# A two-layer graph attention kernel: step 2's norm, flags and adjacency moved, layer 0's mask behind the sums with u, and one maximum as guard

## The chip, the cores and the metric

The kernel runs on one core of a Trainium2 chip. A core has five engines that run at the same time, each through its own list of instructions in order: TensorE (PE, with its weight loads PEld), VectorE (DVE), ScalarE (ACT), GpSimd (POOL) and SyncE (SP, here only a queue that issues DMA transfers; ACT issues some too). Engines wait for each other by semaphores. The metric is the device time of one execution in microseconds (us), lower is better.

## The reference

The input is x, 64 graphs of 256 nodes with 512 features in float32, and a Boolean adjacency of 256 x 256 for each graph. There are two pre-norm attention layers:

```python
h = jnp.maximum(_layernorm(x, axis=-1), 0.0)
x = x + _L0_gnn_ref(h, adj, Wq, Wk, Wv, Wo, bo)
h = jnp.maximum(_layernorm(x, axis=-1), 0.0)
x = x + _L1_gnn_ref(h, adj, gamma, beta, w_qkv, w_out, b_out)
```

Layer 0 has 4 heads of 64, a score outside the adjacency becomes the lowest float, and a node with no neighbour at all therefore attends evenly to all nodes. Layer 1 has 8 heads of 64, a second layernorm with gamma and beta inside, and a mask of adjacency or identity. Both take a softmax over the allowed nodes and project the heads back to 512 features with a bias. All of it is float32.

## The kernel before

**Steps and tiles.** `fast_path` treats two graphs at a time: 512 rows as NT = 4 tiles of 128 x 512, 32 steps in all. Each step goes through layer 0 and layer 1. In a steady period the second layer of step s is mixed with the first layer of step s + 2 and the end of layer 0 of step s + 1, so that PE always has matmuls.

**Projections by seven products.** A projection (q and k together, v, output) is computed as seven half-size products n = 1 to 7 instead of eight (Strassen and Winograd), in the order `SET = (1, 6, 5, 2, 7, 3, 4)`. A product is accumulated in a PSUM bank by PE (L841 for q and k and layer 1's v, L922 for layer 0's v, L938 for the output). It is then taken out by `evacuate` (ACT L775 for n = 1, L783 for n = 2; DVE L777 for n = 6, L779 for 5, L781 for 7, L785 for 3, L787 for 4) or, for the output, by `accumulate` (ACT L794; DVE L796, L798, L800, L803, L805; and three additions of u on POOL, L809: `SUM_U`). Products 3 and 4 go on in the banks that 5 and 7 have used, after the evacuation of 5 and 7; 2 goes on in the bank of 1. The products need sums of quadrants of the inputs (L404 for the weights, once, by `weight_sum`; L407 to L412 on POOL for h and for the attention's result).

**Attention.** PE makes the scores of a pair of heads (L994), DVE adds the mask (L1017), ACT takes the exponential (L1022). No maximum is subtracted. Keys lie on the partitions, so the sums over keys are made in steps: POOL adds the two halves of the keys (`key_halves`, L1029, into the single buffer pd), DVE transposes in 32 x 32 blocks (L1035) and reduces (L1042), then transposes the result (L1095) and sums and inverts (`key_sums`, L1103, L1106). The inverse sums are written to DRAM as a line (SP, L1113) and read back broadcast into the output's tile (SP, `inverse_in`, L1124); PE weighs the values (L1065, L994) and POOL multiplies by the inverse (`normalise`, L1142).

**Guard.** The softmax without a maximum is safe if no sum and no inverse is too large. `key_sums` writes one number for each unit of two pairs of heads into `extremes`; after the last step its overall maximum is compared with a limit, and a slower `general_path` runs only if it is exceeded. L1107 makes that number: a `tensor_tensor_reduce` that adds sums and inverses and takes the maximum, which appears as a custom instruction and a read of the accumulator (97 times).

**Norm and adjacency of layer 0.** `norm0` takes mean and variance of a tile of x on DVE (L615, L616); POOL then makes the scale and the shift of each row (L648, `row_scales` L625 to L627), and ACT applies them (`scale_row`, L631). `norm1` and `norm1_rest` do the like for layer 1 (L615/L616 twice, ACT L672/L673, POOL L688, L689, L625 to L627). h is transposed for PE by DVE in 32 x 32 blocks (`turn_blocks`, L724) and by 16 DMA transfers on SP (`move_blocks`, L736), then copied into place by ACT (L747); the first and some last steps do this on PE (L700, L706).
From step 2 on, the adjacency bytes are packed by POOL (`adjacency_pack`, L532, 3.08 us) and transposed by DVE (`adjacency_turn`, L540, 16 instructions of 0.235 us). `neighbours` (DVE, L559, two) finds the nodes that have a neighbour, `neighbours_line` (DVE, L568, four) turns these flags into a row, and `neighbours_spread` (SP, L575, three transfers) spreads it to all partitions. `mask0` (POOL, L549 and twice L602, 3.4 us) makes the mask of layer 0 from the transposed adjacency and the flags, `mask1` (L549 and twice L610) that of layer 1.

**The order of the work.** It is written out by hand. Every piece is put in a list by `at(period, place, fn, ...)`, the list is sorted by period and place, and the pieces are emitted in that order, so each of PE, DVE, ACT and POOL executes its instructions in that order. A period is 6.4 units of place (6.2 for those before the first, `FIRST`), one unit being about 15 us. An instruction that waits holds up all that stand behind it on its engine. Most places are the same in every step; steps 0, 1 and 2 have places of their own, since in the warm-up (the first 190 us or so) the weights are also transposed by PE (L468, copied by L473) and their sums made (L404: four each of wqk, wo0 and wo1, of wqkv's Q, K and V, and of wv).

Tiles come from pools with a tag and a number of buffers. A tile that reuses a buffer waits until its former content has been read. Which tag a tile has therefore also sets when a load can start.

Of the kernel before, what the change touches and what calls it, by code (L numbers as in the profile page):

```python
# [8 lines left out]
FP = mybir.dt.float32  # L9
# [4 lines left out]
ALU = mybir.AluOpType  # L14
# [301 lines left out]
def fast_path(  # L316
# [19 lines left out]
    nc = tc.nc  # L336
    P = 128
    B, N, D = x.shape
    DH = 64
    G = 2  # L340
    NSTEP = B // G
    NIC = N // P
    NT = G * NIC
# [9 lines left out]
    act = ctx.enter_context(tc.tile_pool(name="act", bufs=1))  # L353
    sm = ctx.enter_context(tc.tile_pool(name="sm", bufs=2))
# [64 lines left out]
    wo0 = const.tile([P, NB, HP0, HD], FP, name="wo0")  # L419
    wqkv1 = const.tile([P, NB, HC, 3, H1], FP, name="wqkv1")  # L420
# [92 lines left out]
    both = act.tile([P, 2, NIC, P, NT], U8, name="both")  # L513
# [99 lines left out]
    def moments(mv, src, t):  # L613
        bs = stat.tile([P, 6], FP, name="bs")
        nc.vector.bn_stats(bs, src[:, t, :])  # L615
        nc.vector.bn_aggr(mv[:, t, 0:2], bs)  # L616
# [47 lines left out]
    def norm1(s, k):  # L664
        st, x1, t = S[s], S[s]["xt"], NORM1[k]
        if k == 0:
            st["mv"] = stat.tile([P, NT, 3], FP, name="mv1", bufs=2)
            st["mean"] = stat.tile([P, NT, 2], FP, name="mg", bufs=2)
            st["h"] = act.tile([P, NT, D], FP, name="h", tag="h" if by_tensor(s, 1) else "turned")
        mv, h = st["mv"], st["h"]  # L670
        moments(mv, x1, t)
        nc.scalar.mul(mv[:, t, 2:3], mv[:, t, 0:1], -1.0)  # L672
        nc.scalar.activation(h[:, t, :], x1[:, t, :], AF.Relu, bias=mv[:, t, 2:3])  # L673
# [40 lines left out]
    def by_tensor(s, lyr):  # L714

        return s == 0 or s == (1, NSTEP - 1)[lyr]
# [262 lines left out]
    units = [0]  # L979
# [108 lines left out]
    def turn_sums(s, lyr, prs):  # L1088

        st = S[s]  # L1090
        part = st.pop(("part", lyr, prs))[:, :len(prs)].rearrange("p i b -> p (i b)")
        nb = 32 * len(prs)
        keys = sm.tile([P, 7, 2 * 32], FP, name="keys", tag="turned_p", bufs=1)[:32, :, :nb]
        for k in range(4):
            nc.vector.transpose(keys[:, k], part[32 * k:32 * (k + 1)])  # L1095
        st["keys", lyr, prs] = keys

    def key_sums(s, lyr, prs):

        st = S[s]  # L1100
        keys = st.pop(("keys", lyr, prs))
        sums, inv, both = (keys[:, k] for k in (4, 5, 6))
        nc.vector.tensor_reduce(  # L1103
            sums, keys[:, :4].rearrange("b k q -> b q k"), axis=mybir.AxisListType.X, op=ALU.add
        )
        nc.vector.reciprocal(inv, sums)  # L1106
        nc.vector.tensor_tensor_reduce(  # L1107
            out=both, in0=sums, in1=inv, scale=1.0, scalar=0.0, op0=ALU.add, op1=ALU.max,
            accum_out=extremes[:32, units[0]:units[0] + 1],
        )  # L1110
        units[0] += 1
        line = st["line", lyr, prs] = dram.tile([len(prs), 2, T], FP, name="line")
        nc.sync.dma_start(  # L1113
            line.rearrange("i e (b q) -> (e b) i q", q=32), inv.rearrange("b (i q) -> b i q", q=32)
        )
# [36 lines left out]
    def at(period, place, fn, *args):  # L1152
        events.append((period * (PERIOD if period >= 0 else FIRST) + place, len(events), fn, args))
# [68 lines left out]
    AT_X, AT_C0, AT_QK, AT_Q0, AT_V0, AT_H1, AT_Z = 2.0, 3.0, 3.5, 4.5, 5.5, 6.06, 6.2  # L1222
# [8 lines left out]
    p = NSTEP - 2  # L1231
# [9 lines left out]
    FIRST_C0, FIRST_Q0, FIRST_V0, FIRST_H1 = 3.0, 3.64, 4.64, 5.2  # L1241
# [5 lines left out]
    for s in range(NSTEP):  # L1247

        p = s - 2
        if s == 1:  # L1250
            p -= 3.93 / FIRST
        at(p - 1 if s != 1 else -2, 3.2 if s == 1 else 5.7 if s < 3 else AT_H1 + 0.01, load_h, s)
        at(p - 1 if s != 1 else -2, 3.2 if s == 1 else 5.7 if s < 3 else 1.3, load_adjacency, s)
        if s < 2:
            at(p, (2.0, 2.4)[s], adjacency_cast, s)
            at(p, (FIRST_Q0 + 0.1425, 3.583)[s], adjacency_transpose, s)
        else:
            at(*((p, 0.45) if s == 2 else (p - 1, 4.9)), adjacency_pack, s)
        for t in range(NT):
            at(p, (0.5 + 0.4 * t, 1.95 + 0.1395 * t)[s] if s < 2 else (0.95, 1.05, 1.2, 1.35)[t], norm0, s, t)  # L1260
            if s == 0:
                at(p, 0.95 + 0.4 * t, first_scale, t)
            else:
                at(p, (2.6 + 0.1 * t, 2.35 + 0.001 * t)[s - 1] if s < 3 else 1.6 + 0.001 * t, scale_row, s, t)
            if not by_tensor(s, 0):
                at(p, AT_X - 0.00035 + 0.00001 * t if s > 2 else (2.6, 2.601, 2.72, 2.721)[t], turn_blocks, s, 0, t)
        if not by_tensor(s, 0):
            at(p, AT_X - 0.00031 if s > 2 else 3.0, move_blocks, s)
        for g in range(G):
            if s < 3:  # L1270
                at(p, (1.8, 2.7, 0.1)[s] + 0.001 * g, neighbours, s, g)
            else:
                at(p - 1, AT_Q0 - 0.0009, neighbours, s, g)
        if s < 2:
            at(p, (2.9, 2.72)[s], neighbours_rows, s)
            at(p, (FIRST_Q0 + 0.285, 3.59)[s], neighbours_turn, s)
        else:
            at(p, 2.3 if s == 2 else 0.05, neighbours_line, s)
            at(p, 2.31 if s == 2 else 0.051, neighbours_spread, s)
        for a in range(NQ if s > 1 else 0):  # L1280
            place = (2.05, 2.2, 2.86, 2.9)[a] if s == 2 else AT_X - 0.00031 if a > 2 else 1 + (a + 4) / 7 - 0.0005
            at(p, place, adjacency_turn, s, a)
        at(p, (FIRST_Q0 + 0.3, 3.74)[s] if s < 2 else 3.1, mask0, s)
        at(p, (FIRST_Q0 + 0.31, 4.43)[s] if s < 2 else 5.85, mask1, s)
        if s == 0:
            at(p, FIRST_C0, first_transposes)
        else:
# [9 lines left out]
        if s < 2:  # L1297
            for t in range(NT):
                place = (FIRST_V0 + 0.14 * t - (0 if t else 0.0005), (4.31, 5.02, 5.16, 5.31)[t])[s]
# [7 lines left out]
        p = s - 1  # L1307
# [20 lines left out]
        for k in range(NT):  # L1328
            at(p, ((2.901, 3.041, 3.181, 3.321), (2.99919, 2.99933, 2.99947, 2.99961), (3.79, 3.8, 3.94, 3.95))[edge][k], norm1, s, k)
            at(  # L1330
                p, ((3.042, 3.182, 3.322, 3.323), (2.99948, 3.2, 3.3, 3.45), (4.08, 4.22, 4.23, 4.37))[edge][k],
                norm1_rest, s, k,
            )
            at(*((0, 3.6 + 0.001 * k), (p, 6.5 + 0.1 * k), (p, 5.6 + 0.01 * k))[edge], second_bias, s, k)
            place = ((3.6112, 3.6113, 3.7502, 3.7503)[k], 3.6 + 0.01 * k, AT_Q0 + (-0.0002, -0.00019, 0.0002, 0.00021)[k])[edge]
            at(p, place, scale_row, s, NORM1[k])
            if edge == 2:
                at(p, AT_Q0 + (0.15, 0.16, 0.29, 0.3)[k], turn_blocks, s, 1, NORM1[k])
# [8 lines left out]
        p = s  # L1347
        if s < NSTEP - 1:
# [3 lines left out]
            p, place = (s + 1, 1.0) if s < NSTEP - 2 else (s, LAST_QK + 2)  # L1352
# [5 lines left out]
        else:  # L1358
            p = s - 1
# [15 lines left out]
    at(-3, 5.71, lambda: gbr.append(first_weights()))  # L1375
    for i in range(4):
        at(-2, 3.01, weight_sum, nc.vector, wqk0, i)
        at(0, 0.9, weight_sum, nc.gpsimd, wo0, i)
    for n, (p, place) in enumerate(((-2, 4.0), (-2, 4.0), (-1, 0.0), (-1, 1.1))):
        at(p, place, lambda n=n: blocks.update({n: weight_load(n)}))  # L1380
    at(-2, FIRST_V0 + 0.2, lambda: gamma_beta(gbr[0]))
    for i in range(16):

        place = (
            *(3.3 - 3.93 + (1 + k) / 7 - 0.0005 for k in range(7)), 0.5205,
            *(0.53 + 0.14 * (k + 1) - 0.0005 for k in range(4)), *(FIRST + (2 + k) / 7 - 0.0005 for k in range(4)),
        )[i]
        at(-1, place, lambda i=i: weight_block(blocks[i // 4], i // 4, i % 4))
    for i in range(4):
        at(-1, 0.1 + 0.01 * i, weight_sum, nc.vector, wqkv1[:, :, :, 0, :], i)  # L1390
        at(-1, 0.54 + 0.0001 * i, weight_sum, nc.gpsimd, wqkv1[:, :, :, 1, :], i)
        at(0, 0.65, weight_sum, nc.gpsimd, wqkv1[:, :, :, 2, :], i)
        at(0, (4.7, 4.701, 4.702, 5.55)[i], weight_sum, nc.gpsimd, wo1, i)
        at(0, 3.61, weight_sum, nc.gpsimd, wv0, i)
# [54 lines left out]
```

## Time and profile before

| | us |
|---|---|
| median of 3 runs | 3095.58 (3095.57 to 3095.6) |
| profiled execution, own time | 3096.28 |
| its span | 3094.5 |
| PE busy | 3072.8 (99%) |
| DVE busy | 2555.7 (83%) |
| POOL busy | 2301.9 (74%) |
| ACT busy | 1207.2 (39%) |

The span is the time from the first to the last instruction in the trace. TensorE had its full clock throughout. In a line of the timeline the columns are start, busy time, engine, line, operation, output and inputs by the program's names, their sizes, the number of instructions taken together (x), and in brackets the idle time of the engine ahead of it and what ended it. In the view of waits the columns are total, times and longest.

### The profile page before, as it was taken

Reading aid. Unit: us, or ns where it says so; the run is one execution under the profiler, and the core shown is the slowest. Engines: PE = TensorE matmul, PEld = TensorE weight load, DVE = VectorE, ACT = ScalarE, POOL = GpSimd, SP = SyncE. Lnnn points to the kernel's source line nnn. Section 1 sums busy time; section 2 is a strip of 40 time slices with the busy share of each in tenths; the row PEclk is TensorE's granted clock in tenths of the full one; section 3 lists DMA queues with packets and bytes.
Section 4 is the critical chain, followed back from the end, with each engine's and each line's share of the span. In section 5 each row is a group of like instructions: output and inputs, shape, how many; then the busy total and the mean of one; then the engine's idle time right before and its main releaser. Section 6 shows DMA issues by size and latency. Waiting matters only on the chain.

```text
span 3094.5 us, 55510 instructions
## 1 busy us (share of the span) xinstructions
PE 3072.8 (99%) x20122; PEld 2528.8 (82%) x20122; DVE 2555.7 (83%) x4851; ACT 1207.2 (39%) x2136; POOL 2301.9 (74%) x2128
## 2 busy tenths in 40 slices
PE   9999999999999999999999999999999999999998
PEld 7778888888888888888888888888888888888887
DVE  6888888888888888888888888888888888888766
ACT  4424343343433344343434334343334444343431
POOL 7887876777777878778787777777787877778753
PEclk9999999999999999999999999999999999999999
DMA  4232222331323322223323233132232222331311
GB/s 140 62 94 80 74 83 74 100 94 54 91 73 92 94 71 79 80 79 94 93 61 88 72 97 94 56 92 73 89 94 80 74 83 73 101 92 53 92 34 50
DMA packets 187591, 251.22 MB, mean 81 GB/s; under 512 B 58088, under 2 KB 78192, under 8 KB 187312
## 3 DMA queue, kind: packets, MB, share of 16 engines
q1 hardware_dynamic: 123776, 179.93, 20.0%
q10 hardware_dynamic: 63536, 67.68, 7.5%
q8 instruction: 162, 2.65, 0.4%
q14 instruction: 117, 0.96, 0.1%
HBM read 128.59 MB, written 34.34 MB: 53 GB/s over the span
## 4 chain that ended last, share of the span: by engine, by line
PE 93%; POOL 3%; DVE 3%; DMA 1%; issue 1%; ACT 0%; SPq 0%; ACTq 0%; DVEq 0%; POOLq 0%
PE mm L841 36%; PE mm L938 17%; PE mm L922 11%; PE sc L994 8%; PE mm L888 6%; PE sc L1065 6%; PE mm L1065 5%; PE mm L994 2%; POOL pd L1029 1%; PE mm L871 1%; DMA h<-blocks 0%; PE mm L964 0%; DVE bs L615 0%; DMA out_dram<-xt 0%; POOL xt L809 0%
## 5 line engine op out<-in xcount | busy, mean ns | idle before, releaser
L841 PE MATMUL mm<-hT,wqkv 128*128 128x256 f32 x3584 | 789.6, 380 | 2.9 <-DVE qk L781 2.1
L841 PEld LDWEIGHTS mm<-hT,wqkv 128*128 128x128 f32 x3584 | 677.1, 190 | 107.2 <-issue 11.8
L1029 POOL TENSOR_TENSOR pd<-p 128x512 f32<-128x512 f32 x383 | 479.3, 1273 | 254.7 <-ACT p L1022 199.1
L938 PE MATMUL mm<-wo,oT 128*128 128x256 f32 x2632 | 579.1, 379 | 1.4 <-DVE v L787 1.2
L938 PEld LDWEIGHTS mm<-wo,oT 128*128 128x128 f32 x2632 | 499.5, 190 | 71.2 <-POOL xt L510 1.5
L1022 ACT ACTIVATE p<-p 128x512 f32<-128x512 f32 x766 | 440.9, 626 | 122.9 <-DVE p L1017 111.4
L1017 DVE TENSOR_TENSOR p<-sc,n 128x512 f32<-128x512 f32 x579 | 363.0, 682 | 111.5 <-PE sc L994 111.5
L841 PE MATMUL mm<-hT,wqk 128*128 128x256 f32 x1792 | 399.0, 382 | 0.0
L922 PE MATMUL mm<-wqkv,hT 128*128 128x256 f32 x1792 | 396.0, 381 | 1.0 <-DVE v L779 0.6
L922 PEld LDWEIGHTS mm<-wqkv,hT 128*128 128x128 f32 x1792 | 337.6, 190 | 57.1 <-issue 10.3
L841 PEld LDWEIGHTS mm<-hT,wqk 128*128 128x128 f32 x1792 | 338.5, 191 | 55.7 <-issue 10.3
L994 PE MATMUL sc<-qk 64*128 64x256 f32 x2320 | 294.7, 385 | 2.2 <-DVE p L1017 2.2
L809 POOL TENSOR_TENSOR xt<-xt,u 128x512 f32<-128x512 f32 x183 | 230.5, 1273 | 66.8 <-DVE xt L798 37.4
L994 PEld LDWEIGHTS sc<-qk 64*128 64x128 f32 x2320 | 218.3, 186 | 63.8 <-issue 27.9
L1035 DVE STREAM_TRANSPOSE turned_p<-pd 128x1024 f32<-128x1024 f32 x192 | 237.1, 1235 | 33.7 <-POOL pd L1029 33.7
L631 ACT ACTIVATE h<-h,mr,r 128x512 f32<-128x512 f32 x252 | 187.6, 803 | 169.8 <-POOL mr L627 169.8
L1142 POOL TENSOR_TENSOR oT<-oT 128x512 f32<-128x512 f32 x188 | 239.9, 1276 | 0.1
L1042 DVE TENSOR_REDUCE part<-turned_p 128x32 f32<-128x1024 f32 x192 | 233.2, 1214 | 4.4
L1065 PE MATMUL sc<-p,v 128*32 128x256 f32 x3152 | 190.8, 382 | 0.0
L888 PE MATMUL mm<-hT,wv 128*128 128x256 f32 x840 | 188.5, 382 | 0.2 <-ACT vT L775 0.2
L794 ACT COPY u<-mm 128x512 f32<-128x512 f32 x62 | 36.3, 585 | 369.9 <-PE mm L938 218.5
L888 PEld LDWEIGHTS mm<-hT,wv 128*128 128x128 f32 x840 | 156.6, 190 | 27.3 <-ACT vT L775 6.6
(155 smaller groups left out, 4458.3 us busy)
## 6 DMA issues: line engine op xcount, KB each, us to landing
h<-blocks SPq DMA_DIRECT2D x960, 64.0 KB, 2.0
oT<-line SPq DMA_DIRECT2D x376, 128.0 KB, 3.0
h<-in_x_dram SPq DMA_DIRECT2D x31, 1024.0 KB, 7.5
xt<-in_x_dram ACTq DMA_DIRECT2D x60, 512.0 KB, 4.3
out_dram<-xt SPq DMA_DIRECT2D x31, 512.0 KB, 3.1
out_dram<-xt ACTq DMA_DIRECT2D x31, 512.0 KB, 4.4
v<-values ACTq DMA_DIRECT2D x480, 32.0 KB, 1.9
ne<-ne SPq DMA_DIRECT2D x90, 64.0 KB, 2.0
```

The source lines that it names most:

```text
L841: nc.tensor.matmul(bank[:, k, :], w[:, wa, c, k, a * P:(a + 1) * P], st["hT"][:, ba, c, :], start=first and (k, c) == (0, 0), stop=(k, c) ...
L888: nc.tensor.matmul(bank, wv0[:, wa, c, :], st["hT"][:, ba, c, :], start=first and c == 0, stop=c == HC - 1, skip_group_check=True,)
L922: nc.tensor.matmul(bank[:, t, :], st["hT"][:, ba, c, t * P:(t + 1) * P], wqkv1[:, wa, c, 2, :], start=first and (t, c) == (0, 0), stop=(t, ...
L938: nc.tensor.matmul(bank[:, t, :], oT[:, ba, c, t * P:(t + 1) * P], w[:, wa, c, :], start=first and (t, c) == (0, 0), stop=(t, c) == (NIC - ...
L994: nc.tensor.matmul(sc[g][e][:, kc, :], qk[rows, 1, k0:k0 + P], qk[rows, 0, g * N:(g + 1) * N], start=True, stop=True,)
L1017: nc.vector.tensor_tensor(p[e][:, g], sc[e], neg[:, :, g, :], ALU.add)
L1022: nc.scalar.activation(p[e][:, g], p[e][:, g], AF.Exp, scale=SCALE)
L1029: nc.gpsimd.tensor_tensor(st["pd"][:, e], p[e][:, :, 0, :], p[e][:, :, 1, :], ALU.add)
L1035: nc.vector.transpose(st["turned_p"], st.pop("pd").rearrange("p e g (b k) -> p (e g b) k", k=32))
L1042: nc.vector.tensor_reduce(st["part", lyr, prs][:, i], st.pop("turned_p"), axis=mybir.AxisListType.X, op=ALU.add)
L1065: nc.tensor.matmul(po[r0:r0 + 32, g, :], (st["v1"][:, g * NIC + kc, pr * P + r0:pr * P + r0 + Q] if lyr else st["v0"][:, r0 // Q, pr, g * ...
L1142: nc.gpsimd.tensor_tensor(dst, dst, invb, ALU.mult)
```

## The change

It has three parts.

1. **Step 2's own preparation for layer 0 takes other places.** Its load of h is issued about one period earlier on SP (for that, layer 1's h of step 0 moves from the tag "h" to the tag "turned"). The four `norm0`, the two `neighbours`, `neighbours_line` and `neighbours_spread`, and 12 of the 16 transposes of `adjacency_turn` on DVE, the row scales, `adjacency_pack` and `mask0` on POOL, and the four `scale_row` on ACT all come earlier in their engines' lists; so does the second mask of step 1. To make room, some weight sums move: the fourth K sum on DVE and on POOL goes later, and those of wo0 come earlier.
2. **Layer 0's mask of steps 3 to 31** (`mask0`, place 3.1) goes to place 3.58, behind the three additions of u (L809) of the step before on POOL.
3. **The guard** takes one `tensor_reduce` with a maximum over sums and inverses together, in place of the `tensor_tensor_reduce` over their sum; its scratch tile has six rows instead of seven.

```diff
-            st["h"] = act.tile([P, NT, D], FP, name="h", tag="h" if by_tensor(s, 1) else "turned")
+            st["h"] = act.tile([P, NT, D], FP, name="h", tag="h" if s == NSTEP - 1 else "turned")
...
-        keys = sm.tile([P, 7, 2 * 32], FP, name="keys", tag="turned_p", bufs=1)[:32, :, :nb]
+        keys = sm.tile([P, 6, 2 * 32], FP, name="keys", tag="turned_p", bufs=1)[:32, :, :nb]
...
-        sums, inv, both = (keys[:, k] for k in (4, 5, 6))
+        sums, inv = keys[:, 4], keys[:, 5]
...
-        nc.vector.tensor_tensor_reduce(
-            out=both, in0=sums, in1=inv, scale=1.0, scalar=0.0, op0=ALU.add, op1=ALU.max,
-            accum_out=extremes[:32, units[0]:units[0] + 1],
+        nc.vector.tensor_reduce(
+            extremes[:32, units[0]:units[0] + 1], keys[:, 4:6], axis=mybir.AxisListType.XY, op=ALU.max
         )
...
-        at(p - 1 if s != 1 else -2, 3.2 if s == 1 else 5.7 if s < 3 else AT_H1 + 0.01, load_h, s)
-        at(p - 1 if s != 1 else -2, 3.2 if s == 1 else 5.7 if s < 3 else 1.3, load_adjacency, s)
+        at(*((p - 1, 5.7), (-2, 3.2), (-2, 5.3))[s] if s < 3 else (p - 1, AT_H1 + 0.01), load_h, s)
+        at(*((p - 1, 5.7), (-2, 3.2), (-2, 5.35))[s] if s < 3 else (p - 1, 1.3), load_adjacency, s)
...
-            at(*((p, 0.45) if s == 2 else (p - 1, 4.9)), adjacency_pack, s)
+            at(*((p, -5.82) if s == 2 else (p - 1, 4.9)), adjacency_pack, s)
...
-            at(p, (0.5 + 0.4 * t, 1.95 + 0.1395 * t)[s] if s < 2 else (0.95, 1.05, 1.2, 1.35)[t], norm0, s, t)
+            at(p, (0.5 + 0.4 * t, 1.95 + 0.1395 * t, -6.3 + 0.01 * t)[s] if s < 3 else (0.95, 1.05, 1.2, 1.35)[t], norm0, s, t)
...
-                at(p, (2.6 + 0.1 * t, 2.35 + 0.001 * t)[s - 1] if s < 3 else 1.6 + 0.001 * t, scale_row, s, t)
+                at(p, (2.6 + 0.1 * t, (-5.8, -5.799, -5.6, -5.599)[t])[s - 1] if s < 3 else 1.6 + 0.001 * t, scale_row, s, t)
...
-                at(p, (1.8, 2.7, 0.1)[s] + 0.001 * g, neighbours, s, g)
+                at(p, (1.8, 2.7, -5.8)[s] + 0.001 * g, neighbours, s, g)
...
-            at(p, 2.3 if s == 2 else 0.05, neighbours_line, s)
-            at(p, 2.31 if s == 2 else 0.051, neighbours_spread, s)
+            at(p, -4.99 if s == 2 else 0.05, neighbours_line, s)
+            at(p, -4.98 if s == 2 else 0.051, neighbours_spread, s)
...
-            place = (2.05, 2.2, 2.86, 2.9)[a] if s == 2 else AT_X - 0.00031 if a > 2 else 1 + (a + 4) / 7 - 0.0005
+            place = (-5.0, -4.999, -4.998, 0.29)[a] if s == 2 else AT_X - 0.00031 if a > 2 else 1 + (a + 4) / 7 - 0.0005
...
-        at(p, (FIRST_Q0 + 0.3, 3.74)[s] if s < 2 else 3.1, mask0, s)
-        at(p, (FIRST_Q0 + 0.31, 4.43)[s] if s < 2 else 5.85, mask1, s)
+        at(p, (FIRST_Q0 + 0.3, 3.74, 1.9)[s] if s < 3 else 3.58, mask0, s)
+        at(p, (FIRST_Q0 + 0.31, 4.153)[s] if s < 2 else 5.85, mask1, s)
...
-        at(0, 0.9, weight_sum, nc.gpsimd, wo0, i)
+        at(-1, 1.21, weight_sum, nc.gpsimd, wo0, i)
...
-        at(-1, 0.1 + 0.01 * i, weight_sum, nc.vector, wqkv1[:, :, :, 0, :], i)
-        at(-1, 0.54 + 0.0001 * i, weight_sum, nc.gpsimd, wqkv1[:, :, :, 1, :], i)
+        at(-1, 0.41 if i > 2 else 0.1 + 0.01 * i, weight_sum, nc.vector, wqkv1[:, :, :, 0, :], i)
+        at(-1, 1.22 if i > 2 else 0.54 + 0.0001 * i, weight_sum, nc.gpsimd, wqkv1[:, :, :, 1, :], i)
```

## The prediction

> **What bounds the kernel now.** I read the page first, then PE's waits, then the timeline step by step. The page's busy line:
>
> ```profile
> PE 3072.8 (99%) x20122; PEld 2528.8 (82%) x20122; DVE 2555.7 (83%) x4851; ACT 1207.2 (39%) x2136; POOL 2301.9 (74%) x2128
> ```
>
> PE is nearly always busy, but a matmul's end is modelled, so a busy share doesn't say how much can be won. The start of the same block of matmuls, layer 1's first product with wqk, in two successive middle steps (timeline of PE) says it better:
>
> ```profile
> 1009.93 12.35 PE L841 MATMUL mm<-hT,wqk 128*128 128x256 f32 x56
> 1104.86 12.35 PE L841 MATMUL mm<-hT,wqk 128*128 128x256 f32 x56
> ```
>
> A step takes 94.93 us, with no gap on PE: middle steps are bound by TensorE, and VectorE (DVE) and POOL only have to be in time. An edit can win only where PE waits. PE's waits (us in total, times, longest):
>
> ```profile
> PE sc L994 <- DVE p L1017: 2.2, 2, 1.3
> PE mm L841 <- DVE qk L781: 2.1, 4, 0.7
> PE mm L841 <- DVE qk L779: 0.8, 1, 0.8
> PE mm L938 <- DVE v L787: 1.2, 1, 1.2
> PE mm L922 <- DVE v L779: 0.6, 1, 0.6
> ```
>
> All are rare, so they belong to single steps. The view shows each some 0.2 us short (the modelled ends), so I size a loss by comparing a block's start-to-start time with the same block of a middle step. The windows view gives both; the first number is the length, the next four pairs are PE, its loads, DVE and ACT:
>
> ```profile
> 103.72:109.54 5.82, 4.52 (x37) 3.21 (x33) 5.68 (x14) 2.20 (x4) 4.13 (x8) 1.00 0.32 92
> 1006.28:1009.93 3.65, 3.65 (x36) 3.03 (x32) 2.48 (x5) 3.51 (x6) 3.57 (x4) 1.00 0.00 0
> 109.54:122.57 13.03, 12.43 (x57) 10.58 (x57) 12.79 (x27) 6.71 (x12) 11.53 (x12) 1.00 0.07 16
> 1067.19:1079.39 12.20, 12.20 (x59) 10.75 (x58) 8.47 (x11) 4.23 (x8) 10.95 (x11) 1.00 0.55 153
> 122.57:130.54 7.97, 6.55 (x29) 5.08 (x28) 7.71 (x17) 0.58 (x1) 7.80 (x7) 1.00 0.35 83
> 1079.39:1085.43 6.04, 6.04 (x29) 5.32 (x28) 5.22 (x8) 0.58 (x1) 5.87 (x6) 1.00 0.00 0
> ```
>
> From 103.7 to 130.5 us DVE is busy 26.2 of 26.8 us, and PE loses 5.82 - 3.65 = 2.17, 13.03 - 12.20 = 0.83 and 7.97 - 6.04 = 1.93: 4.93 us. This is where step 2's norm, flags and turns sit on DVE. The timeline shows the first loss directly: four norm pairs (L615/L616, 0.80 us each) stand before the mask that PE's second scores wait for.
>
> ```profile
> 107.17 2.45 DVE L1017 TENSOR_TENSOR p<-sc,n 128x512 f32<-128x512 f32 x4
> 107.88 1.73 PE L994 MATMUL sc<-qk 64*128 64x256 f32 x8 [1.30 <-DVE p L1017]
> ```
>
> The same comparison finds three more families. At 61.42 a block takes 1.03 instead of 0.44: L871 waits for L785, queued behind four weight sums L404 (0.58). In steps 3, 4 and 6 the blocks at 228.58, 324.30 and 515.1 lose 0.79, 0.49 and 0.81 at L781. And from 162.2 to 190.9 PE loses 0.40 + 0.72 + 2.00 = 3.12 behind an unbroken POOL chain from the third sum with u (133.66) to the key halves L1029 (183.2). For step 3 the timeline reads:
>
> ```profile
> 229.49 2.28 POOL L602 TENSOR_TENSOR n<-n,ne 128x512 bf16<-128x512 bf16 x2
> 231.74 3.78 POOL L809 TENSOR_TENSOR xt<-xt,u 128x512 f32<-128x512 f32 x3
> 234.32 0.69 DVE L615 BATCH_NORM_STATS2 bs<-xt 128x6 f32<-128x512 f32 x1 [1.18 <-POOL xt L809]
> ```
>
> The layer-1 norm waits 1.18 us for sums that waited for layer 0's mask.
>
> **What the Trainium skill says.** "Perfetto Trace Analysis", Identifying the Most-Contended Engine: matmul busy share is a bad measure[...]; this trace agrees (99% busy, yet some 15 us of stalls). "SBUF — State Buffer", Who interferes with whom: DVE and GpSimd share a port pair under an exclusive lock. The trace agrees: the L404 at 57.90 took 1.64 us instead of 0.69 while POOL's L1142 ran, and one guard maximum, L1107 at 170.58, took 2.70 us and ended with POOL's L677. "DMA: Bandwidth & Descriptors", Issuing engines are not separate DMA queues: all transfers interleave on the same 16 engines, so the early load of h competes with whatever is in flight; its rows here: 1 MB in 7.5 us, oT<-line in 3.0.
>
> **The change part by part.** Durations are from the timeline; the order in which each engine's instructions stand was compared before and after, and PE's order and waits don't change.
>
> *Norm of step 2.* Four L615/L616 pairs (3.2 us of DVE) go from 103.4-107.2 to behind L779 (ends 53.63), where DVE idled 3.67 us before L781 (57.29): they end at about 56.9. They need h, now asked for at 41.2 instead of 84.3, one line transfer earlier on SP; at 7.5 us it lands at about 49, so 4 us of cover. If it came after 53.7, L781 and every evacuation behind it would be late. POOL's four small instructions (1.85 us) go in at 57.7, before the normalisation L1142. ACT's four L631 (2.9 us) go in as pairs at 62.7 and 65.3, beside PE's weight products; ACT is 39% busy, some 0.3 us of delay.
>
> *L404, L785.* Only three sums now stand before L785, but POOL's r (1.03 us) may lock the port. L785 comes about 0.7 earlier or as now: gain 0 to 0.58, taken 0.45.
>
> *Flags, turns.* Two L559 (1.27 us) move from 87.8 to about 62.4, after L787; twelve L540 (0.235 each) and four L568 (0.30) move in front of L1017 at 81.57, where DVE idled 4.4 us: 76.97 + 0.2 + 2.8 + 1.2 = 81.0, and PE frees the mask's scores at about 81.0. This is the tightest place: slack 0.2 us, and each microsecond over costs one. Four L540 (0.94) go before L779 at 92.02 (idle 1.04). Three spreads L575 (2.0 us) go ahead of the third line transfer on SP at about 81; what waits for that has over 5 us.
>
> *POOL moves.* The pack (3.08) goes from 92.45 to about 66, three K sums behind it, wo0's four and the fourth K sum to about 79; mask 1 of step 1 before L851 (1 us each way) and mask 0 of step 2 (3.4) from 126 to about 102. POOL idles there; the row scales of step 0's norm (L688 on) move by under 0.3 us. Taken as nothing; up to 1 us if the key halves slip.
>
> *What is won at 104-130.* L1017 becomes ready with PE (104.3), 2.17 gone. With eight L540 and four L568 (3.1 us) out of 111.9-118.2, L779 comes before PE needs it: 0.83 gone. With eight L540 (2.0) out of 123.6-125.6, the turns L724 fit the idle 2.4 us of DVE and L787, L796 and L798 are in time to 0.3 us: 1.93 gone, bounds 1.6 to 1.93. PE's layer 0 block at 130.5 starts at about 125. The POOL chain behind it starts with it and is as long as before, its weight sums unmoved: 3.12 stays.
>
> *Mask 0 behind the sums, steps 3 on.* Two sums (2.5 us) no longer wait for 3.3 us of mask, so L615 starts when DVE is free (233.1 instead of 234.3), and L781 comes before PE needs it: 0.79 + 0.49 + 0.81 = 2.09 gone, bounds 0 (if the late inputs of those steps bind) and 2.09. In middle steps the mask then ends at about 1093.9, and next on POOL are
>
> ```profile
> 1093.73 0.20 POOL L688 TENSOR_SCALAR ve<-mv 128x4 f32<-128x4 f32 x1 [2.96 <-DVE mv L616]
> 1098.16 0.20 POOL L689 TENSOR_TENSOR ve<-ve,mg 128x4 f32<-128x4 f32 x1 [4.23 <-DVE mg L616]
> ```
>
> L688 may slip 0.2 us, L689 has 4 us left: nothing. Without that cover it would cost 29 times the overrun.
>
> *Guard.* L1107 (0.411 mean) with its accumulator read (0.071), 97 times, becomes one reduction of 32x128 into one value. Nearest rows: L1103 to 32x32 from 32x128, 0.374; a 128x100 reduction to one column, 0.257. "VectorE: DVE Perf Modes", The TRN2 errata, prices 58 + 128 cycles at 0.96 GHz: an estimate of 0.19, and says the row under-predicts. I take 0.28, so 0.2 x 97 = 19 us less of DVE. None of it is on PE's path in a middle step: gain 0, bounds 0 and 0.4 (the block at 324.30 had an L1107 of 1.35 us). Not reading two SBUF inputs, it should no longer be held by POOL; no trace shows this yet.
>
> **Sum.** 0.45 + 4.93 + 2.09 = 7.5 us. Against the profiled execution's own 3096.28 (span 3094.5) that gives 3088.8 (span 3087.0); the median of the runs is 0.7 lower: 3088.1, 0.24% less. A measurement here can tell about 0.2%, 6.2 us, from no change: the boundary is 3089.4.
>
> **Rivals.** (a) Steps 3, 4 and 6 stay late: ACT comes late there too, its load of xt waiting for a store. For: steps 2, 3 and 5 see that delay; against: the only wait before L615 is for POOL. 7.5 - 2.1 = 5.4, so 3090.2; chance 0.17. (b) The 3.12 also goes, since the unlocked guard and an emptier DVE let POOL's chain run faster: for, the 2.70 us maximum; against, POOL is continuous there. 3085.0; 0.17. (c) A new wait in the warm-up: the flags and turns overrun L1017 at 81, or h's load holds back the two line transfers at 42.65 that L1142 at 52.94 needs. An overrun of 3 to 4 us: about 3091.5; 0.13. (d) Slower: mask 0 behind the sums holds the row scales, so ACT's L631, the turned blocks and PE's next block, in each of 29 steps. Price: the overrun past 4 us of slack at L689; it needs 0.47 us each (13.7 less the 7.5 won) to leave 3101.8; 1 us each gives 3095.6 - 7.5 + 29 = 3117. The rows above speak against it; 0.06. The forecast has 0.47.
>
> **The numbers.** The forecast with its bounds is 3087 to 3089.3. Range 3085.0 to 3092.0 takes in (a), most of (b) and (c), and leaves out (d) and the ends. Faster: nearly all of 0.47, 0.17, a little of (a): 0.66. Slower: 0.06, and 0.01 for a worse (c): 0.07. Same: 0.27.
>
> **What would show it.** Right: L1017 no longer ahead in PE's waits, the block from 103.7 at 3.65, L615 without POOL's 1.18, a step still 94.93, L1107's successor near 0.28. Wrong: PE idle at 57, 81 or 92 before L781, L1017, L779; a middle step longer than 94.93; the 162-191 stalls grown or gone.

## The result, and the profile after

The changed kernel takes 3088.67 us (median of 14 runs, 3087.52 to 3089.65), against 3095.78 before (14 runs beside them, 3094.80 to 3100.49). The ratio is 0.9976, with a 95% interval from 0.9967 to 0.9984: 7.1 us less, where 7.5 was forecast. A second set of runs of the same kernel gave 3088.31 against 3095.81, ratio 0.9975 (0.9965 to 0.9985). The profiled execution has its span at 3087.4 us, 7.1 less than before.

The page's busy line after:

```profile
PE 3068.8 (99%) x20122; PEld 2528.5 (82%) x20122; DVE 2539.7 (82%) x4754; ACT 1207.4 (39%) x2136; POOL 2308.9 (75%) x2128
```

DVE has 97 instructions and 16 us less; a middle step still takes 94.92 us, so hardly any of these 16 us show. PE's waits after (us in total, times, longest):

```profile
PE mm L758 <- ACT h L657: 7.9, 2, 7.7
PE sc L994 <- DVE p L1017: 1.0, 1, 1.0
PE mm L841 <- DVE qk L779: 0.9, 1, 0.9
PE mm L841 <- DVE qk L781: 0.7, 1, 0.7
PE mm L922 <- ACT v L775: 0.4, 1, 0.4
PE mm L841 <- POOL hT L410: 0.3, 1, 0.3
PE mm L888 <- ACT vT L775: 0.3, 1, 0.3
```

The first line is the wait for the first loads, 6.9 us before. One of the two waits for L1017 is gone (the one left is at the end of the kernel), L781 has one wait instead of four, and L787 and the wait of L922 for L779 are gone. The windows view for the same three blocks as before, and for step 3's block (behind the length come PE, its loads, DVE, ACT and POOL, each with its number of instructions, then the granted clock and the load of the DMA engines):

```profile
103.72:107.38 3.66, 3.66 (x37) 3.03 (x33) 2.49 (x5) 2.29 (x4) 1.92 (x2) 1.00 0.14 49
107.38:119.57 12.19, 12.19 (x58) 10.74 (x57) 10.51 (x15) 3.92 (x8) 11.28 (x11) 1.00 0.08 28
119.57:125.61 6.04, 6.04 (x29) 5.32 (x28) 5.48 (x9) 0.59 (x1) 5.17 (x5) 1.00 0.38 89
223.77:235.95 12.18, 12.18 (x57) 10.45 (x55) 11.79 (x29) 4.54 (x10) 7.03 (x7) 1.00 0.15 44
```

All four have the length that they have in a middle step, and PE (the second number) is busy through each. Where DVE was busy 26.2 of 26.8 us, it is now busy 18.5 of 21.9.

Block by block, from start to start in the two traces:

| place in the trace before | forecast | measured |
|---|---|---|
| 61-64 us, L871 behind L785 | -0.45 | -0.68 |
| 104-131 us, L1017, L779, L787 | -4.93 | -4.94 |
| steps 3, 4 and 6, L781 | -2.09 | -2.12 |
| 162-191 us, POOL's chain | 0 | +0.07 |
| start of the kernel, up to 18 us | 0 | +0.69 |
| some blocks in steps 2, 5, 10 and 14 | 0 | -0.48 |
| end of the kernel | 0 | +0.36 |

The first four rows gain 7.67, 0.2 more than forecast; the last three give 0.57 back, which makes 7.1. In the first of these ACT's fourth scaling of step 0 (L657), which waits for the first loads, started at 10.39 us instead of 9.41; 0.29 of these 0.98 us came back by 18 us.

The tightest place that the forecast named, ahead of L1017 at 81 us, held (timeline of DVE):

```profile
77.01 2.94 DVE L540 STREAM_TRANSPOSE both<-both 32x64 f32<-32x64 f32 x12
79.96 1.24 DVE L568 STREAM_TRANSPOSE ne<-any_of 32x128 f32<-32x128 f32 x4
81.51 2.48 DVE L1017 TENSOR_TENSOR p<-sc,n 128x512 f32<-128x512 f32 x4 [0.30 <-PE sc L994]
```

DVE was done 0.30 us before PE gave it the scores; 0.2 was forecast. The guard, in the view of one line before and after (ns: shortest, median, longest):

```profile
L1107 DVE CUSTOM_DVE_ANT_0 keys<-keys x97: 211/323/2704, 41.2 to 3058.6; 32x64 f32<-32x64 f32 x95, 32x32 f32<-32x32 f32 x2
L1107 DVE DVE_READ_ACCUMULATOR2_ANT extremes<- x97: 70/71/72, 42.5 to 3059.0; 32x1 f32 x97
```

```profile
L1107 DVE TENSOR_REDUCE extremes<-keys x97: 207/274/276, 42.0 to 3051.1; 32x1 f32<-32x128 f32 x95, 32x1 f32<-32x64 f32 x2
```

The forecast of 0.28 holds (0.274). At its best the old form was faster by itself (0.211), but it was drawn out to as much as 2.70; the new one never takes longer than 0.276. That is what the Trainium skill, "SBUF — State Buffer", Who interferes with whom, says of a DVE instruction with two SBUF inputs beside POOL's reads, and of a reduction, which keeps off the shared ports. The trace before agrees: the 2.70 us from 170.58 end at 173.28, 0.08 us after a POOL instruction (L677).

### The profile page after: what moved, and what is told of

It reads as the page before. It is cut to its first block, busy times and chain, and to the rows that moved or that the text cites. A ratio compares the mean times of both kernels' runs of the same rounds, so it can differ in the third digit from the quotient of the medians.

```text
span 3087.4 us, 55474 instructions
## 1 busy us (share of the span) xinstructions
PE 3068.8 (99%) x20122; PEld 2528.5 (82%) x20122; DVE 2539.7 (82%) x4754; ACT 1207.4 (39%) x2136; POOL 2308.9 (75%) x2128
## 4 chain that ended last, share of the span: by engine, by line
PE 97%; POOL 2%; DVE 1%; issue 0%; DMA 0%; ACT 0%; ACTq 0%; SPq 0%; POOLq 0%; DVEq 0%
PE mm L841 37%; PE mm L938 18%; PE mm L922 13%; PE sc L994 9%; PE sc L1065 6%; PE mm L888 6%; PE mm L1065 5%; PE mm L994 3%; PE mm L871 1%; PE mm L964 0%; POOL pd L1029 0%; PE mm L468 0%; PE mm L700 0%; POOL xt L809 0%; POOL wqk L677 0%
## 5 line engine op out<-in xcount | busy, mean ns | idle before, releaser
L841 PE MATMUL mm<-hT,wqkv 128*128 128x256 f32 x3584 | 789.1, 380 | 1.9 <-DVE qk L779 0.9
L841 PEld LDWEIGHTS mm<-hT,wqkv 128*128 128x128 f32 x3584 | 677.3, 190 | 105.6 <-issue 11.8
L1029 POOL TENSOR_TENSOR pd<-p 128x512 f32<-128x512 f32 x383 | 479.6, 1274 | 257.5 <-ACT p L1022 199.6
L1017 DVE TENSOR_TENSOR p<-sc,n 128x512 f32<-128x512 f32 x579 | 362.6, 681 | 113.8 <-PE sc L994 113.6
L841 PE MATMUL mm<-hT,wqk 128*128 128x256 f32 x1792 | 398.7, 382 | 0.2
L922 PE MATMUL mm<-wqkv,hT 128*128 128x256 f32 x1792 | 395.5, 381 | 0.4 <-ACT v L775 0.4
L841 PEld LDWEIGHTS mm<-hT,wqk 128*128 128x128 f32 x1792 | 338.3, 191 | 55.8 <-issue 10.3
L922 PEld LDWEIGHTS mm<-wqkv,hT 128*128 128x128 f32 x1792 | 337.8, 190 | 55.7 <-issue 10.3
L809 POOL TENSOR_TENSOR xt<-xt,u 128x512 f32<-128x512 f32 x183 | 233.1, 1274 | 140.1 <-DVE xt L803 67.5
L994 PE MATMUL sc<-qk 64*128 64x256 f32 x2320 | 293.3, 385 | 1.0 <-DVE p L1017 1.0
L994 PEld LDWEIGHTS sc<-qk 64*128 64x128 f32 x2320 | 217.8, 186 | 61.5 <-issue 27.6
L1141 POOL TENSOR_TENSOR oT<-oT 128x512 f32<-128x512 f32 x188 | 240.3, 1278 | 0.6 <-DMA oT<-line 0.6
L888 PE MATMUL mm<-hT,wv 128*128 128x256 f32 x840 | 188.5, 382 | 0.3 <-ACT vT L775 0.3
L888 PEld LDWEIGHTS mm<-hT,wv 128*128 128x128 f32 x840 | 156.6, 190 | 27.3 <-ACT vT L775 6.6
```

What stands on the lines that cost most here:

```text
L809: (nc.vector if last else nc.gpsimd).tensor_tensor(r, r, u, ALU.add)
L841: nc.tensor.matmul(bank[:, k, :], w[:, wa, c, k, a * P:(a + 1) * P], st["hT"][:, ba, c, :], start=first and (k, c) == (0, 0), stop=(k, c) ...
L888: nc.tensor.matmul(bank, wv0[:, wa, c, :], st["hT"][:, ba, c, :], start=first and c == 0, stop=c == HC - 1, skip_group_check=True,)
L922: nc.tensor.matmul(bank[:, t, :], st["hT"][:, ba, c, t * P:(t + 1) * P], wqkv1[:, wa, c, 2, :], start=first and (t, c) == (0, 0), stop=(t, ...
L994: nc.tensor.matmul(sc[g][e][:, kc, :], qk[rows, 1, k0:k0 + P], qk[rows, 0, g * N:(g + 1) * N], start=True, stop=True,)
L1017: nc.vector.tensor_tensor(p[e][:, g], sc[e], neg[:, :, g, :], ALU.add)
```

## The experiments

### One part at a time

**Step 2's own preparation alone.** The kernel after, with the mask and the guard of before:

```diff
-        at(p, (FIRST_Q0 + 0.3, 3.74, 1.9)[s] if s < 3 else 3.58, mask0, s)
+        at(p, (FIRST_Q0 + 0.3, 3.74, 1.9)[s] if s < 3 else 3.1, mask0, s)
...
-        nc.vector.tensor_reduce(
-            extremes[:32, units[0]:units[0] + 1], keys[:, 4:6], axis=mybir.AxisListType.XY, op=ALU.max
-        )
+        nc.vector.tensor_tensor_reduce(
+            out=both, in0=sums, in1=inv, scale=1.0, scalar=0.0, op0=ALU.add, op1=ALU.max,
+            accum_out=extremes[:32, units[0]:units[0] + 1],
+        )
```

> Part 1 alone (step 2's own preparation moved; layer 0's mask and the guard as before). Theory: the stalls at 61, 104, 110 and 123 us go, 0.6 + 4.9 = 5.5 us, while the blocks at 229, 324 and 515 us stay 0.8, 0.5 and 0.8 us long, so 5.5 us less than before. Rival, that the guard or the mask helps in the warm-up too: under 4.5 us. The first loads vary by some 0.7 us from execution to execution.

Measured: 3090.08 against 3096.19, ratio 0.9978 (0.9970 to 0.9987), 6.1 us less. In the trace the stalls at 61, 104, 110 and 123 us are gone (-0.68, -2.17, -0.84, -1.93, in all 5.6), and steps 3, 4 and 6 still lose 0.49, 0.82 and 0.82. The theory holds; this part carries most of the gain.

**The mask behind the sums alone.** The kernel before, with one line changed:

```diff
-        at(p, (FIRST_Q0 + 0.3, 3.74)[s] if s < 2 else 3.1, mask0, s)
+        at(p, (FIRST_Q0 + 0.3, 3.74)[s] if s < 2 else 3.1 if s < 3 else 3.58, mask0, s)
```

> Part 2 alone (layer 0's mask of steps 3 on behind the sums with u). Theory: only the three blocks of steps 3, 4 and 6 get shorter, 0.8 + 0.5 + 0.8 = 2.1 us less. Rival (late inputs bind there): 0, with L615 waiting for something else than POOL. A middle step stays at 94.92 us under both.

Measured: 3094.69 against 3096.19, ratio 0.9996 (0.9988 to 1.0004). The total can't be told from no change, but the trace can: step 3's block lost its 0.80, step 4's its 0.50 and step 6's its 0.82, 2.12 together, and L615 no longer waits for POOL. The same trace answers the rival of late inputs. In it a block shortly ahead of step 6's (L922 at 495) was late for its input, 12.93 instead of 12.19 (12.46 in the trace before), and yet step 6's block took 12.18. The windows of both blocks here, and below them in the experiment with the guard alone:

```profile
495.14:508.07 12.93, 12.46 (x59) 10.66 (x57) 8.63 (x11) 4.29 (x8) 9.25 (x8) 1.00 0.51 151
514.30:526.48 12.18, 12.18 (x57) 10.45 (x55) 11.79 (x30) 4.53 (x10) 7.00 (x7) 1.00 0.15 45
495.86:508.89 13.03, 12.46 (x58) 10.66 (x57) 8.63 (x12) 4.30 (x8) 9.25 (x8) 1.00 0.53 150
515.13:528.06 12.93, 12.45 (x58) 10.37 (x56) 11.47 (x28) 4.53 (x10) 7.00 (x7) 1.00 0.12 42
```

In the experiment with the norm alone, below, it was the other way: mask ahead of the sums, no late block, and step 6's block took 12.18 too. With the guard alone there were both, 13.03 and then 12.93. So in these traces step 6's stall needed both, a late input and the mask ahead of the sums; taking either away removed it. How much the three blocks lose differs between executions: with the mask ahead of the sums 0.65 to 2.1 us together in five traces (before, step 2 alone, guard, norm, flags and turns), with the mask behind them nothing in six.

**The guard alone.** The kernel before, with the new maximum:

```diff
-        nc.vector.tensor_tensor_reduce(
-            out=both, in0=sums, in1=inv, scale=1.0, scalar=0.0, op0=ALU.add, op1=ALU.max,
-            accum_out=extremes[:32, units[0]:units[0] + 1],
-        )
+        nc.vector.tensor_reduce(
+            extremes[:32, units[0]:units[0] + 1], keys[:, 4:6], axis=mybir.AxisListType.XY, op=ALU.max
+        )
```

> Part 3 alone (the guard as one maximum). Theory: 97 times 0.2 us less of DVE, no path through it, 0 to 0.4 us less; the stalls of 3.1 us between 162 and 191 us stay. Rival (the guard holds the port that POOL wants, so POOL's chain is longer for it): those 3.1 us shrink by over 1 us. No maximum takes over 0.3 us, where one took 2.7 before.

Measured: 3094.48 against 3096.19, ratio 0.9994 (0.9985 to 1.0002). Its trace has a span of 3094.4, 0.1 less than before. The stall at 172 us (0.72) that followed the maximum of 2.70 us is gone, but the next block is longer by 0.68. The new maximum is not what did this. In the trace of the mask alone, with the old maximum, the one at this place took 0.21 us, and the blocks changed by -0.69 and +0.70 as well; with the norm, the turns or all of step 2 moved alone it was 0.22 or 0.23, with the same result. So the 2.70 us belong to one execution, and without them the wait only moves, since POOL's chain holds PE up a little later. The three stalls together lose 3.15 instead of 3.12; rival (b) falls.

The mask's place acts on the guard too. In the trace of the mask alone the old maximum reads

```profile
L1107 DVE CUSTOM_DVE_ANT_0 keys<-keys x97: 211/213/1270, 41.2 to 3056.9; 32x64 f32<-32x64 f32 x95, 32x32 f32<-32x32 f32 x2
```

Only 3 of the 97 took over 0.4 us, 29 in the trace before, where most of these stood beside POOL's sums with u (L809). DVE's busy time falls by 14.5 us with the mask alone, by 14.4 with the guard alone and by 16.0 with the whole change. Whether the 1.7 us by which the medians differ are more than chance these runs don't settle.

### Step 2's moves taken apart

**The norm alone.** The kernel before, with these of the change's lines: the tag of h, `load_h`, `norm0`, `scale_row` and DVE's fourth K sum.

```diff
+            at(p, (0.5 + 0.4 * t, 1.95 + 0.1395 * t, -6.3 + 0.01 * t)[s] if s < 3 else (0.95, 1.05, 1.2, 1.35)[t], norm0, s, t)
...
+                at(p, (2.6 + 0.1 * t, (-5.8, -5.799, -5.6, -5.599)[t])[s - 1] if s < 3 else 1.6 + 0.001 * t, scale_row, s, t)
...
+        at(-1, 0.41 if i > 2 else 0.1 + 0.01 * i, weight_sum, nc.vector, wqkv1[:, :, :, 0, :], i)
```

> Of part 1 only the norm: load of h, four norms, row scales, scaling and the fourth sum on DVE; flags, turns, masks, POOL's sums and the guard as before. Theory of separate stalls: 2.17 at L1017 and 0.6 at L785 go, 0.8 and 1.9 stay: 2.7 us less. Rival, one backlog of DVE from 104 to 130 us that shrinks by all the work removed: 3.2 + 0.6 = 3.8 us less, with the later stalls cut by 1 us.

Measured: 3092.49 against 3096.19, ratio 0.9988 (0.9982 to 0.9995). The medians differ by 3.7, which would be the rival's figure. The windows say otherwise:

```profile
102.72:106.37 3.65, 3.65 (x36) 3.03 (x32) 2.80 (x6) 2.29 (x4) 2.48 (x4) 1.00 0.09 30
106.37:119.31 12.94, 12.43 (x58) 10.59 (x57) 12.71 (x26) 3.92 (x8) 11.54 (x12) 1.00 0.15 48
119.31:127.28 7.97, 6.55 (x29) 5.08 (x28) 7.71 (x17) 0.58 (x1) 7.80 (x7) 1.00 0.35 82
```

The first block is whole again, and the next two are as long as before (12.94 against 13.03, 7.97 against 7.97) although DVE had 3.2 us less to do ahead of them. The stalls are separate: once PE starts 2.2 us earlier, it asks for the next evacuation 2.2 us earlier as well. At 61 and 104 us 0.68 and 2.16 are gone, 2.84 in all. Most of what this execution gained beyond that lies in steps 3 to 6: step 5's input was in time, so the 0.27, 0.20 and 0.82 of steps 5 and 6 are missing, and 0.60 in step 3.

**The flags and turns alone.** The kernel after, with the tag, `load_h`, `norm0`, `scale_row`, DVE's fourth K sum, the guard and the masks of steps 3 on as before; of what stays of the change these lines matter most (the masks of steps 1 and 2, POOL's sums, `load_adjacency` and `neighbours_spread` stay too):

```diff
+            at(*((p, -5.82) if s == 2 else (p - 1, 4.9)), adjacency_pack, s)
...
+                at(p, (1.8, 2.7, -5.8)[s] + 0.001 * g, neighbours, s, g)
...
+            at(p, -4.99 if s == 2 else 0.05, neighbours_line, s)
...
+            place = (-5.0, -4.999, -4.998, 0.29)[a] if s == 2 else AT_X - 0.00031 if a > 2 else 1 + (a + 4) / 7 - 0.0005
```

> Of part 1 only the flags, the adjacency's turns and pack, the masks of steps 1 and 2 and POOL's sums; step 2's norm with its load and scaling, DVE's fourth K sum, the guard and the mask of steps 3 on as before. Theory of separate stalls: 0.8 and 1.9 at 110 and 123 us go, 2.17 at L1017 and 0.6 at L785 stay: 2.8 us less than before. Rival, one backlog of DVE that only its total sets: the 2.17 shrinks too and over 3.5 us go.

Measured: 3094.82 against 3096.01, ratio 0.9996 (0.9988 to 1.0005): less than either theory. In the trace the blocks at 110 and 123 us lose 0.61 and 1.78 us of their stalls, near the theory's 0.8 and 1.9, and L1017's stall shrinks by 0.64. But 1.3 us come back at 61 us, where four weight sums and POOL's mask of step 1 now run side by side:

```profile
57.40 5.18 DVE L404 TENSOR_TENSOR wqkv<-wqkv 128x512 f32<-128x512 f32 x4
62.50 0.68 DVE L785 TENSOR_TENSOR qk<-mm,qk 128x512 f32<-128x512 f32 x1
```

Four sums took 5.18 us; before they took 3.89 in the same place. Each of the four ended 0.54 or 0.55 us after an instruction of POOL had ended, the last three after those of the mask. In the kernel after, three took 2.21: there the row scales of step 2's norm stand ahead of this mask on POOL, and it starts at 62.45, behind the sums. Another 1.0 us comes back at 160 us, where the wait of L888 for ACT's L775 is 1.2; which move made POOL's chain later there was not tested. So the flags and turns alone cost something at 61 us that the whole change doesn't pay; whether the fourth sum or POOL's order spares it these runs don't separate.

**All 16 turns ahead of L1017.**

```diff
-            place = (-5.0, -4.999, -4.998, 0.29)[a] if s == 2 else AT_X - 0.00031 if a > 2 else 1 + (a + 4) / 7 - 0.0005
+            place = (-5.0, -4.999, -4.998, -4.997)[a] if s == 2 else AT_X - 0.00031 if a > 2 else 1 + (a + 4) / 7 - 0.0005
```

> The kernel after, with all 16 turns L540 of step 2 ahead of L1017 at 81.5 us instead of 12 (1.0 us more of DVE there). DVE idled 0.3 us before that L1017 in the kernel after. Theory (the tightest place): PE's scores L994 wait 0.7 us there, and nothing gives it back: 0.7 us more than after. Rival: the four score banks give PE room, and nothing is lost.

Measured: 3089.22 (ratio 0.9977, 0.9969 to 0.9986, against before), beside 3088.67 for the kernel after. PE's scores L994 lost nothing. The late DVE reached PE one step on, through L706 (half of hT) and POOL's sums of it:

```profile
87.16 1.99 PE L841 MATMUL mm<-hT,wqkv 128*128 128x256 f32 x8 [0.20 <-POOL hT L410]
```

That block took 4.02 us instead of 3.56: 0.46 lost, where the theory said 0.7 and named another waiter. The place is as tight as the forecast had it; its price per microsecond is lower.

### How much cover the moved mask has

Both kernels are the kernel after, with the two multiplications of layer 0's mask repeated in steps 3 to 31, four times and six times, and the same result:

```diff
-            nc.gpsimd.tensor_tensor(v, v, st["ne"], ALU.mult)
+            for _ in range(4 if s > 2 else 1):
+                nc.gpsimd.tensor_tensor(v, v, st["ne"], ALU.mult)
```

> The kernel after, with the two multiplications by ne (L602) of layer 0's mask made four times each in steps 3 to 31, the same result: 6.9 us more of POOL behind the sums in each step. The row scales L689 had 4.6 us of cover in a middle step of after, so they come 2.3 us late. Theory of the forecast's slower case: each microsecond over costs one on PE, a step of 97.2 us and 65 us more in all. Rival: behind L689 there is cover of its own (ACT's L631, POOL's sums L407 to L412 and the halves L1029 are needed 1.5 to 4 us later), a step stays within 0.3 us of 94.92.

> As the kernel with four multiplications for each of layer 0's mask, but six: 11.5 us more of POOL in each of steps 3 to 31 than the kernel after. With 6.9 us more, a step grew by 0.93. Theory (cover of 6.0 us up to the key halves L1029 some 35 us later, then each microsecond over costs one): a step of 94.92 + 5.5 = 100.4 us, 160 us more in all. Rival (part of the excess is taken up again and again by POOL's gaps): under 4 us a step.

Measured: 3118.00 (four runs, ratio 1.0070, 1.0055 to 1.0086) and 3270.39 (two runs, 1.0562, 1.0543 to 1.0581), that is 29.3 and 181.7 us more than the kernel after. Lines in these two stand one further down than in the kernel after (L842 is its L841). PE's waits in the first:

```profile
PE mm L842 <- DVE qk L782: 20.5, 29, 1.0
```

and in the second:

```profile
PE mm L842 <- POOL hT L410: 113.0, 30, 4.8
```

The timeline of POOL shows how late the row scales are, in the kernel after:

```profile
1081.42 1.27 POOL L809 TENSOR_TENSOR xt<-xt,u 128x512 f32<-128x512 f32 x1 [1.78 <-DVE xt L803]
...
1091.00 0.20 POOL L689 TENSOR_TENSOR ve<-ve,mg 128x4 f32<-128x4 f32 x1 [4.23 <-DVE mg L616]
```

and with four multiplications for each:

```profile
1090.73 1.27 POOL L810 TENSOR_TENSOR xt<-xt,u 128x512 f32<-128x512 f32 x1 [1.79 <-DVE xt L804]
...
1093.21 9.75 POOL L603 TENSOR_TENSOR n<-n,ne 128x512 bf16<-128x512 bf16 x8
1103.04 0.20 POOL L689 TENSOR_SCALAR ve<-mv 128x4 f32<-128x4 f32 x1
1103.32 0.20 POOL L690 TENSOR_TENSOR ve<-ve,mg 128x4 f32<-128x4 f32 x1
```

From the third sum with u to the second row scale it is 12.59 us instead of 9.58, so the row scale came 3.0 us later; a typical step took 0.93 longer (95.85). With six it came 8.0 later, and a step took 100.8 to 101.1 in 19 of 28 cases, mostly 5.9 longer. Both leave 2.1 us of cover behind that row scale, on top of some 4.5 us in front of it (the eight multiplications took 9.75 us where two took 2.29, 7.5 more, and 3.0 of it was late), so about 6.6 us in all; beyond that a microsecond costs one. The theory of the forecast's slower case was wrong in its first microseconds (it counted only the cover at L689) and right in its slope. Which instruction waits changes: at first it is DVE's transposition of the halves L1029, late because POOL's work follows without a gap from the mask to them; further on it is PE's second product, which needs POOL's sums L410.

In the second kernel the wait is not all that PE loses. In each step it waits about 3.8 us for L410, and around the end of this wait the granted clock is at half for 3.4 or 6.8 us (windows view of 6.13 us behind one wait, and of as long a stretch in the same block a little later; the clock is the number behind the five engines):

```profile
1059.67:1065.80 6.13, 6.13 (x14) 4.88 (x15) 1.90 (x3) 4.98 (x9) 6.13 (x6) 0.50 0.01 3
1070.00:1076.13 6.13, 6.13 (x30) 5.25 (x29) 4.03 (x5) 0.37 (x1) 5.72 (x6) 1.00 0.44 103
```

PE was busy through both, with 14 matmuls in the first and 30 in the second. The nine steps with 6.8 us at half clock took 101.9 to 102.7 us. In the 19 others the later block, where PE waits for L782, still takes 12.3 to 12.6 us instead of 12.19. So there POOL's chain sets the length, and the slow clock fills time that PE would otherwise have waited. In the other traces, where no wait behind the start is longer than 1.7 us, the clock stays full from 18 us to PE's last products. That the long wait brings the clock down is likely, but no run tests it.

### The stalls that the change left

Between 157 and 186 us the kernel after still loses 3.2 us, as before. Two experiments take the sums of wo1 out of POOL's chain there.

```diff
-        at(0, (4.7, 4.701, 4.702, 5.55)[i], weight_sum, nc.gpsimd, wo1, i)
+        at(0, (AT_Q0 - 0.0008, AT_Q0 - 0.0007, AT_Q0 - 0.0006, AT_Q0 + 6 / 7)[i], weight_sum, nc.vector, wo1, i)
```

> The kernel after, with layer 1's four sums of wo1 (L404) made by DVE, three in its idle stretch at 140 us and one behind L785 at 156, instead of by POOL at 148 and 162: 5.3 us less in POOL's chain from 138 to 183 us. Theory (POOL's chain of work alone sets the stalls between 157 and 186): the 3.2 us of them go, at most 0.7 come back where DVE's sums delay L1017 at 142.5, so 2.5 to 3.2 us less than after. Rival (ACT's and DVE's own lateness holds PE there too): less than 1.5 us.

Measured: 3087.41 (ratio 0.9972, 0.9961 to 0.9983). The 3.19 us at 157 to 186 go, so POOL's chain is what bound them, but 1.35 come back at L994, more than the 0.7 allowed for. The timeline of DVE in this kernel, and below it the second and third sum one by one among POOL's instructions:

```profile
137.99 4.20 DVE L404 TENSOR_TENSOR wo<-wo 128x512 f32<-128x512 f32 x3
142.10 2.47 DVE L1017 TENSOR_TENSOR p<-sc,n 128x512 f32<-128x512 f32 x4
```

```profile
138.68 1.27 POOL L407 TENSOR_TENSOR hT<-hT 128x512 f32<-128x512 f32 x1
138.70 1.80 DVE L404 TENSOR_TENSOR wo<-wo 128x512 f32<-128x512 f32 x1
140.03 1.60 POOL L410 TENSOR_TENSOR hT<-hT 128x512 f32<-128x512 f32 x1
140.53 1.65 DVE L404 TENSOR_TENSOR wo<-wo 128x512 f32<-128x512 f32 x1
141.59 1.71 POOL L411 TENSOR_TENSOR hT<-hT 128x512 f32<-128x512 f32 x1
```

The three sums took 4.20 us, twice their 0.69 each, and POOL's sums beside them 1.60 and 1.71 instead of 1.27. The engines took turns: the second and third sum on DVE each end 0.55 us after a sum of POOL (139.95 and 141.63), and POOL's L410 and L411 end 1.12 or 1.13 us after one of DVE's (140.50 and 142.18). Both engines pay. The second version puts each sum where the other engine is idle or does something else:

```diff
-        at(0, (4.7, 4.701, 4.702, 5.55)[i], weight_sum, nc.gpsimd, wo1, i)
+        at(0, (1.95, 3.45, AT_Q0 + 6 / 7, 6.1)[i], weight_sum, nc.gpsimd if i < 2 else nc.vector, wo1, i)
```

> The kernel after, with wo1's four sums (L404) in idle stretches that nothing contends for: two on POOL at 105.7 and 127, ahead of its unbroken chain, one on DVE behind L785 at 156, one on DVE at 166. 5.3 us less in POOL's chain as in the last experiment, without its three sums side by side with POOL at 140. Theory: the 3.2 us of stalls between 157 and 186 go and nothing comes back, so 3.2 us less than the kernel after, near 3085.5. Rival: DVE and POOL are so full there that a like stall opens at 105 to 170, less than 1.5 us gained.

> The kernel after, unchanged, beside the last one on the same chip: 7 us less than before, and the time against which the last experiment is read.

Measured: 3085.16 (ratio 0.9964, 0.9950 to 0.9977) beside 3088.31 for the kernel after in the same runs: 3.15 us less. Its longest run (3086.07) is shorter than the shortest of the kernel after (3087.88). All that is left in PE's waits:

```profile
PE mm L758 <- ACT h L657: 7.5, 4, 6.6
PE sc L994 <- DVE p L1017: 1.0, 1, 1.0
PE mm L922 <- ACT v L775: 0.4, 1, 0.4
```

The two DVE sums took 0.68 and 0.67 there, POOL's 1.28 and 1.27: no contention. This version is faster than the kernel before and the kernel after.

## Why the prediction was right

**Sign and size.** 7.5 us was forecast, 7.1 measured, 3088.67 against 3088.1, inside the range. The sum was made in PE's lost time, not in busy time, and each of its large terms came out within 0.1 us (4.94 for 4.93, 2.12 for 2.09). Both sides of this comparison use the one execution before from which the terms were sized, so it shows that the stalls went in full. It doesn't show that they are always that large: with the mask ahead of the sums the traces gave 0.65 to 2.1 for the second.

**L404 and L785.** This term was too small: 0.68 for 0.45, and above its bound of 0.58, since L871's own block gained 0.10 as well. The fear that POOL's r would lock the port over DVE's sums did not come true: the three took 2.21 us, and it was r (L625) that took 1.37 instead of 1.02.

**Norm, flags and turns.** Right, and for the reason given: the experiment with the norm alone shows separate stalls, one for each block, not one backlog. The stretches chosen for them on DVE, 3.67 us at 54 and 4.4 us at 77, were just long enough, with 0.54 and 0.30 us left. For the second this is in part luck. The forecast's sum 76.97 + 0.2 + 2.8 + 1.2 comes to 81.2, not to 81.0, and DVE was done at 81.20. Against scores at 81.0, as it assumed, that is 0.2 too late, but PE gave them at 81.50. How long the early load of h took the trace doesn't say; it was issued at 42.48, and DVE found h there at 54.17 without a wait.

**Mask behind the sums.** Right in its gain. Rival (a) was half right in its cause, as far as step 6 shows it: a late input triggers the stall there, but the mask's place is what turns it into one. For the price in a middle step the forecast looked at the row scales L689 only and took the cover there (4 us) for all of it; the runs show about 6.6.

**Guard.** Duration right, worth on the path nothing that these runs can tell. The 19 us less of DVE were 14.4 with the guard alone, and the moved mask by itself brings nearly as much. Rival (b) is refuted by the guard alone (3.15 us of stalls left) and by wo1's sums, which removed all of them.

**New waits.** Rival (c) didn't come: L1017 at 81 had 0.30 us to spare, and POOL's multiplication behind the line transfers (L1142 before, L1141 after) started at 53.61, no later than 52.94 and the 0.69 of the start. It was near: 1.0 us more of DVE work cost 0.46.

**What the forecast left out.** Step 5's inputs move the span by up to 1 us from execution to execution, and the start of the kernel by more: PE's first L588, at 18.02 us before and 18.71 after, comes between 15.8 and 18.9 us in the 13 traces. Two things vary there. ACT's fourth scaling of step 0 (L657) starts between 9.29 and 10.45 us; the nine traces with the early load of h span this whole range, the four without it 9.41 to 9.93, so nothing shows that the change makes it later. And PE's first matmuls run at half rate: in the trace before, those of L841 start 0.427 us apart up to 15 us and 0.216 apart from 16.7 on, in the trace with wo1 on DVE already 0.216 apart at 11.7. 0.427 is also their distance at half clock in the kernel with six multiplications, so TensorE had its full rate not throughout, but from there on. The 0.6 us between forecast and median are less than this variation; that the total came so near is in part luck.

## What to carry to other kernels

When the engine that bounds a kernel is 99% busy, size each stall as the difference between one block's start-to-start time and the same block's in an undisturbed step; the sum of these predicts the gain, and busy time saved elsewhere (16 us of DVE here) doesn't. Take more than one execution for this: the three stalls at L781 came to 0.65 us in one and to 2.1 in another. Work that is moved into an idle stretch must fit it in time and in ports: two sums on DVE and two on POOL placed apart gave 3.15 us, but three on DVE beside POOL's own gave back 1.35. The cover of a moved step ends where its engine's unbroken chain reaches the next waiter, which here was some 30 us on.

## What the runs showed of the hardware that was not expected

Where DVE and POOL contended, both were drawn out, and they took turns, one instruction at a time: with both at two-input additions of 128x512, DVE's took 1.65 and 1.80 us instead of 0.69 and POOL's 1.60 and 1.71 instead of 1.27, each ending a fixed time after the other's had ended. This agrees with the exclusive lock of the prediction; what it adds is that the engine that came first pays too, at its next instruction. The custom maximum with two inputs took from 0.21 to 2.70 us for 32x64 elements, while the one-input reduction of twice as many elements stayed between 0.207 and 0.277 in all eight traces that have it.

A wait of PE can cost more than its length: around the end of waits of about 3.8 us the granted clock stood at half for 3.4 or 6.8 us, and in the longer case most steps took 102.0 us, 7.1 more than in the kernel after.
